# Four graph layers on one core: layer 2's clamp on POOL, and its next square between two exponentials

## The chip, the cores and the metric

The program runs on one core of a Trainium2 chip. The core has a matrix engine (TensorE, PE in the profile), a vector engine (VectorE, DVE), an engine for activation functions (ScalarE, ACT), a general engine (GpSimd, POOL) and an engine whose queue issues most transfers here (SyncE, SP). Each has its own instruction stream, works in order, and waits on semaphores for the others. [...] the large tiles of this kernel lie in SBUF.

The metric is the device time of one launch in microseconds (us), lower is better.

## The reference

Four layers are applied to x (4096 rows of 64) with one adjacency matrix adj (4096 by 4096). Each layer normalises the rows, cuts them at zero, calls a graph layer and adds its result to x. Layer 0 is a sum over neighbours with a linear map. Layer 1 is a Lorentz attention. Layer 3 weighs each neighbour by powers of one half according to its rank in the row. The change is in layer 2, where every pair of rows (i, j) needs the logarithmic map on the Poincare ball:

```python
sub = mobius_add(-x_i, x_j)
arg = clip(norm(sub), 0, 1 - 1e-5)
log_ij = 2 / lam_i * arctanh(arg) * sub / norm(sub)
agg = einsum('ij,ijc->ic', adj / deg, log_ij)
out = expmap(0, agg @ weight + bias)
```

The kernel takes a weight per pair, arctanh(arg)/norm(sub), out of a quantity that one set of matrix products gives for all pairs. It writes the arctanh as a logarithm. In layer 2 each pair therefore needs a square, a clamp from below, a square root, a logarithm, an inverse square root and a product with adj.

## The kernel before

The columns of adj are cut into 8 blocks of 512 (ib), and the 4096 rows into 16 groups of 256 (g, or J and half). A group is one tile of 128 partitions by 1024 elements: two chunks of 128 rows, each by 512 columns. The distance in layer 2 is symmetric, so only the groups on and above the diagonal are worked through: the list `work` has 72 groups. Row 0 has 16 of them, row 1 has 14, and so on down to 2 in row 7. Of these, 56 are used twice (`d["two"]`): once as they are, and once transposed by TensorE for the mirrored block, whose part is collected in the tile `others`. At each diagonal block the first group is whole and the second (`d["cut"]`) is half a tile.

One group k of layer 2 goes through these steps (the name of the generator, its engine, and the tiles by which the profile shows it):

- `l2_dists`, TensorE: matrix products into a PSUM pair tile (mm<-RT,LT and mm<-RB,LB). There are two such pair tiles.
- `l2_squares`, ScalarE: the square, from PSUM into a buffer v (v<-mm).
- `l2_clamps` (line 1032), VectorE: v = max(v - half, V_MIN), in place (v<-v, TENSOR_SCALAR).
- `l2_signs`, TensorE: two small products into the same PSUM tile, once the square has been read.
- `l2_roots` (line 1050), ScalarE: Ln of v in place (v<-v), Exp with factor 0.5 into a buffer t (t<-v), which is the root, and Exp with factor -0.5 in place (v<-v), which is the inverse root.
- `l2_coshs`, VectorE: t = max(PSUM, ...) + t (t<-mm,t). With this the PSUM pair tile is free.
- `l2_logs`, ScalarE: Ln of t in place (t<-t).
- `l2_pairs`, VectorE: t = min(t, top) * v (t<-t,v).
- `l2_weights`, VectorE: w = t * adj (w<-t,adj). `l2_turns`, TensorE: eight transposes (tr<-ident,t). `l2_weights2`, VectorE: two products (w<-tr,adj) of 512 elements each.
- `l2_sums` and `l2_sums2`, TensorE: the sums over neighbours (acc<-w,HA; 128x512 and 128x256 forms). `l2_gathers` adds the mirrored part to `others` after every second group: on VectorE in rows 1 to 7 (others<-acc,others), on ScalarE in row 0.

The buffers v and t come out of six buffers in turn, so three groups can be under way. All of these are recorded at one line (129) of the profile, by a helper, so the steps are told apart by their tiles.

At the end of each row, `after2` (line 613) turns the sums into the row's output, with small steps on all engines: a power on POOL (r_nn), a tanh on ScalarE between two loads of its table, and then the layer norm of layer 3 (`before3`, line 532) with another power (ln_r) and an addition (x<-x,b) on POOL. In row 0 layer 2's own preparations for later rows (`before2`) run beside the groups. Layer 3 begins while the last rows of layer 2 run: `l3_masks` makes its masks on VectorE.

The order of instructions on each engine is not written by hand. `in_turn` (line 709) holds a list of generators. Each yields the engine of its next step and a function that says when its inputs are ready. A class `Pace` (line 59) keeps an estimate of each engine's time; the generator that could start first goes next. `in_steps` binds several generators into one fixed order: in each step it takes them in the order given, each with its own shift in the number of the group. What the planner emits is kept in that order on each engine, and then runs whenever the semaphores allow. So a step put in another place moves others as well.

In the kernel before, ScalarE's order for group k is: Ln, Exp(0.5), Exp(-0.5), the square of group k+1, and the last Ln of k. VectorE's is: the clamp of k+1, the pair of k, the weight of k, the root's cosh step of k+1 and the two transposed weights of k, with `others` among them.

Of the kernel before, what the change touches and what calls it, by code (L numbers as in the profile page):

```python
# [14 lines left out]
ALU = mybir.AluOpType  # L15
# [35 lines left out]
V_MIN = 2.0**-64  # L51
# [85 lines left out]
def kernel(ctx: ExitStack, tc: tile.TileContext, a: dict, out: bass.AP):  # L137
# [5 lines left out]
    PE, DVE, ACT, POOL = (  # L143
        InOrder(tc, e, pace, name)
        for e, name in (
            (nc.tensor, "PE"), (nc.vector, "DVE"), (nc.scalar, "ACT"), (nc.gpsimd, "POOL"),
        )
    )
# [557 lines left out]
    def latest(*times):  # L706
        return None if None in times else max(times)
# [93 lines left out]
    def pair_buffer(name):  # L801
        return pairp.tile([P, G, W], F32, tag="pair", name=name)
# [148 lines left out]
    half = 0.25 * SC * SC  # L951
# [16 lines left out]
    def part(d, t):  # L968
        return t[:, :, OWN:] if d["cut"] else t
# [1 line left out]
    def targets(d):  # L971
        return slice(d["ib"] * W + (OWN if d["cut"] else 0), (d["ib"] + 1) * W)


    def ago(items, k, n, what):

        return items[k - n].get(what) if k >= n else 0.0
# [44 lines left out]
    def l2_squares():  # L1022
        for k, d in enumerate(work):
            yield "ACT", lambda: latest(
                d.get("dist"), l1[2 * k - SIG].get("summed") if 2 * k < SIG else 0.0,
                ago(work, k, SIG // 2, "paired"),
            )
            d["v"] = pair_buffer("v")
            ACT.activation(part(d, d["v"]), part(d, d["ps"]), AF.Square)
            d["square"] = pace.latest  # L1030

    def l2_clamps():
        for d in work:
            yield "DVE", lambda: d.get("square")
            v = part(d, d["v"])
            DVE.tensor_scalar(v, v, -half, V_MIN, ALU.add, ALU.max)
            d["clamped"] = pace.latest

    def l2_signs():
# [10 lines left out]
    def l2_roots():  # L1050
        for k, d in enumerate(work):
            yield "ACT", lambda: latest(
                d.get("clamped"), opened.get("tables"),
                l1[2 * k + 1 - SIG].get("summed") if 2 * k < SIG else 0.0,
                ago(work, k, SIG // 2, "weighed"), ago(work, k, SIG // 2, "turned"),
            )
            d["t"] = pair_buffer("t")
            v = part(d, d["v"])
            ACT.activation(v, v, AF.Ln)
            ACT.activation(part(d, d["t"]), v, AF.Exp, scale=0.5)  # L1060
            d["root"] = pace.latest
            ACT.activation(v, v, AF.Exp, scale=-0.5)
            d["inverse"] = pace.latest

# [7 lines left out]
    def l2_logs():  # L1072
        for d in work:
            yield "ACT", lambda: d.get("read")
            ACT.activation(part(d, d["t"]), part(d, d["t"]), AF.Ln, scale=2.0 / SC)
            d["log"] = pace.latest

    def l2_pairs():
        for d in work:
            yield "DVE", lambda: latest(d.get("log"), d.get("inverse"))  # L1080
            t = part(d, d["t"])
            DVE.scalar_tensor_tensor(t, t, top, part(d, d["v"]), ALU.min, ALU.mult)
            d["paired"] = pace.latest

    def l2_weights():
        for k, d in enumerate(work):
            yield "DVE", lambda: latest(
                opened.get("second"), d.get("paired"), arrival(d), ago(work, k, 2, "summed")
            )
            if not d["cut"]:  # L1090
                d["w"] = w2["pool"].tile([P, G, W], F32, tag="w", name="w")
            DVE.tensor_mul(part(d, d["w"]), part(d, d["t"]), part(d, d["adj"]))
            d["weighed"] = pace.latest
            used(d)
# [104 lines left out]
    def l2_gathers():  # L1199
        for d in twos:  # L1200
            if d["half"] == 0:
                continue
            yield "DVE" if d["ib"] else "ACT", lambda: d.get("summed2")
            o, acc = w2["others"][:, ws(d["J"])], accs["turned"][0 : D + 1, :]
            if d["ib"] == 0:
                ACT.copy(o, acc)
            else:
                DVE.tensor_add(o, acc, o)
            st["acc_free"][1] = pace.latest
            d["gathered"] = pace.latest  # L1210

    def in_steps(*stages):


        parts = [next(stage[0], None) for stage in stages]
        for step in range(-1, len(work) + 3):
            for n, (gen, behind, many) in enumerate(stages):
                k = step - behind
                for _ in range(many(work[k]) if 0 <= k < len(work) else 0):
                    yield parts[n]  # L1220
                    parts[n] = next(gen, None)
# [55 lines left out]
    def l3_masks():  # L1277
        for k, d in enumerate(l3):
            place, reader = mask_at[k % len(mask_at)]
            yield "DVE", lambda: latest(  # L1280
                arrival(d), reader.get("signed"), ago(l3, k, len(mask_at), "ranked")
            )
            d["m"] = place
            DVE.tensor_scalar(place, d["adj"], 0.0, None, ALU.not_equal)
            d["masked"] = pace.latest
            used(d)
# [7 lines left out]
    def l3_counts():  # L1294


        totals = []
        for h in range(2 * NB):
            half = l3[h * HG : (h + 1) * HG]
            yield "PE", lambda: latest(*(d.get("masked") for d in half)) if spare else None  # L1300
            ps = bank()
            for k in range(KH):
                for r in range(4):
                    c = 4 * k + r
                    PE.matmul(
                        ps[r * Q : (r + 1) * Q, :], pick[:, k, :],
                        half[::-1][c // G]["m"][:, c % G, :],
                        start=(k == 0), stop=(k == KH - 1), skip_group_check=True,
                    )
            yield "DVE", lambda: ready(ps)  # L1310
            totals = (totals if h % 2 else []) + [(1 - h % 2, l3_copy(f"total{h % 2}", ps))]
            yield "PE", lambda: ready(totals[-1][1]) if spare else None
            ps = bank()
            for n, (i, t) in enumerate(totals):
                PE.matmul(
                    ps, spread[:, i, :, :].rearrange("p q c -> p (q c)"), t,
                    start=(n == 0), stop=(n == len(totals) - 1),
                )
            yield "DVE", lambda: latest(ready(ps), ago(l3, h * HG, HG + 1, "ranked"))
            chunks = l3_copy("chunks", ps)  # L1320
            for d in half:
                d["chunks"] = chunks
# [31 lines left out]
    def l3_pass():  # L1354

        for n, pair in enumerate(pairs3):
            while rank_need(pair) is None:
                yield "PE", lambda: first_of(rank_need(pair), sum_need() if sums3 else None)
                if rank_need(pair) is None:
                    l3_sum()  # L1360
            yield "PE", lambda: rank_need(pair)
            l3_rank(pair)
            for _ in range(1 + n % 2):
                if sums3 and sum_need() is not None:
                    yield "PE", sum_need
                    l3_sum()
        while sums3:
            yield "PE", sum_need
            l3_sum()

    def l3_weights():
        n = 0
        for d in l3:
            if d["late"]:
                place, reader = late_at[d["k"]]
                yield "ACT", lambda: latest(d.get("ranked"), reader.get("signed"))
                d["w"] = place
            else:
                yield "ACT", lambda: latest(
                    d.get("ranked"), opened.get("third"),  # L1380
                    ago([e for e in l3 if not e["late"]], n, WT, "summed"),
                )
                d["w"] = now["w3"].tile([P, G, W], BF16, tag="wt", name="wt")
                n += 1
            ACT.activation(d["w"].bitcast(U16), d["ps"], AF.Relu)
            d["read"] = pace.latest
# [8 lines left out]
    def l3_sum():  # L1395
# [22 lines left out]
        if d["last"]:  # L1418
# [8 lines left out]
            (l2_dists(), -1, once), (l2_signs(), 0, once), (l2_sums2(), 2, if_two(1)),  # L1427
            (l2_turns(), 1, lambda d: 2 if d["two"] else 1), (l2_sums(), 1, once),
        ),
        in_steps((l2_logs(), 1, once), (l2_roots(), 0, once), (l2_squares(), -1, once)),  # L1430
        in_steps(
            (l2_clamps(), 0, once), (l2_pairs(), 1, once), (l2_weights(), 1, once),
            (l2_coshs(), 0, once), (l2_weights2(), 1, lambda d: 2 if d["two"] else 1 if d["first"] else 0),
        ),
        l2_gathers(), l3_weights(), l3_pass(), l3_counts(), l3_masks(),
        degree_sums(0, l0), degree_sums(1, l1), constants(),
    ])

# [44 lines left out]
```

## Time and profile before

| what | value |
|---|---|
| time, median of 3 runs | 1198.92 us (1196.69 to 1200.99) |
| the profiled execution's own time | 1196.08 us |
| span of its trace (first to last instruction) | 1194.4 us |
| mean granted TensorE clock | 0.978 of full speed |
| busy: PE / DVE / ACT / POOL | 1077.9 / 950.6 / 800.7 / 118.2 us |
| 487 to 592 us (row 0 of layer 2): PE / DVE / ACT busy of 105 | 95.8 / 94.2 / 92.1 us |
| 592 to 957 us (rows 1 to 7): PE / DVE / ACT busy of 365 | 318.9 / 333.6 / 291.3 us |
| 957 to 1194 us (mostly layer 3): PE / DVE / ACT busy of 237 | 213.9 / 117.6 / 132.7 us |

Layers 0 and 1 fill the first 485 us. The powers r_nn at the row ends of layer 2 start at 604.3, 692.0, 767.9, 832.2, 886.3, 930.3 and 960.3 us on POOL, which makes the rows visible.

In a timeline, a line begins with start and duration in us, then the engine, the line of the kernel, the operation, output<-input, the shapes and the number of instructions merged. In brackets stand the idle time before it and the instruction that ended it. Durations overlap a little: a VectorE instruction of 1.22 us is followed by the next one after 1.13 to 1.15 us, since the end of one runs beside the start of the next.

### The profile page before, as it was taken

What the parts mean: (1) busy time and instruction counts of PE and PEld (TensorE: products, weight loads), DVE (VectorE), ACT (ScalarE), POOL (GpSimd) and SP (SyncE); (2) the same over time, 40 slices, a digit from 0 to 9 for tenths busy, and PEclk for the clock granted to TensorE, in tenths of its full rate; (3) what the DMA queues carried; (4) which work ended last, traced back from release to release, by engine and by line L of the source; (5) the groups of instructions that cost most, each with busy time, mean ns of one, the idle gap of its engine ahead of it and who ended that gap; (6) DMA issues with size and microseconds to landing.
All of it is one profiled execution on the core that took longest, in us unless ns stands there. A gap on an engine that the chain in (4) does not pass through costs nothing.

```text
span 1194.4 us, 15545 instructions
## 1 busy us (share of the span) xinstructions
PE 1077.9 (90%) x5367; PEld 445.8 (37%) x5392; DVE 950.6 (80%) x1571; ACT 800.7 (67%) x1266; POOL 118.2 (10%) x99
## 2 busy tenths in 40 slices
PE   4799999999999999899979979899878779999997
PEld 1234443333333333244434434344433333333332
DVE  7889888869988887698989989898989884555550
ACT  1055456677776766879888798788876675555554
POOL 3123222002000010000010010100010120000000
PEclk9899999999999999899999999999999899999999
DMA  8899999775767764544535535344444398888830
GB/s 307 300 409 388 405 386 329 265 244 184 249 225 244 253 241 157 193 141 159 194 106 177 176 109 198 117 159 159 159 143 141 138 357 319 314 315 310 309 112 9
DMA packets 77190, 271.75 MB, mean 228 GB/s; under 512 B 10040, under 2 KB 11064, under 8 KB 77112
## 3 DMA queue, kind: packets, MB, share of 16 engines
q1 hardware_dynamic: 75456, 270.57, 63.7%
q8 instruction: 42, 0.69, 0.2%
q10 hardware_dynamic: 1656, 0.20, 0.1%
q14 instruction: 36, 0.29, 0.1%
HBM read 269.68 MB, written 1.05 MB: 227 GB/s over the span
## 4 chain that ended last, share of the span: by engine, by line
PE 47%; DVE 25%; ACT 13%; issue 7%; DMA 5%; POOL 2%; SPq 0%; ACTq 0%; DVEq 0%; POOLq 0%
PE acc L129 23%; PE mm L129 16%; PE tr L129 8%; DVE t L129 6%; DVE w L129 6%; DVE dg L129 4%; DMA adj<-in_adjT_dram 4%; ACT wt L129 3%; ACT v L129 3%; ACT t L129 2%; DVE v L129 1%; DVE sig L129 1%; POOL lo_s L129 1%; ACT sig L129 1%; ACT lo_sq L129 1%
## 5 line engine op out<-in xcount | busy, mean ns | idle before, releaser
L129 PE MATMUL acc<-w,HA 128*65 128x256 f32 (+1 forms) x736 | 252.6, 479 | 22.2 <-DVE w L129 13.8
L129 ACT ACTIVATE wt<-mm 128x1024 uint16<-128x1024 f32 x124 | 120.4, 1020 | 93.0 <-PE mm L129 93.0
L129 ACT ACTIVATE v<-v 128x1024 f32<-128x1024 f32 (+1 forms) x144 | 145.3, 1009 | 54.5 <-DVE v L129 52.2
L129 ACT ACTIVATE sig<-mm,att_b,att_a 128x1024 f32<-128x1024 f32 x128 | 148.5, 1202 | 44.2 <-PE mm L129 43.2
L129 DVE TENSOR_TENSOR sig<-sig,adj 128x1024 f32<-128x1024 f32 x128 | 152.5, 1220 | 28.3 <-ACT sig L129 28.1
L129 PE MATMUL acc<-adj,HA 128*64 128x512 f32 x512 | 128.0, 631 | 22.9 <-DVE HA L129 19.4
L129 DVE TENSOR_TENSOR dg<-dg,adj 128x1024 f32<-128x1024 f32 x114 | 139.1, 1220 | 2.0 <-DMA adj<-in_adjT_dram 0.6
L129 PEld LDWEIGHTS acc<-w,HA 128*65 128x65 f32 x736 | 95.8, 140 | 110.5 <-issue 59.5
L129 PE MATMUL mm<-qT,kT 64*128 64x512 f32 x512 | 132.6, 632 | 3.3 <-ACT sig L129 3.3
L129 PE MATMUL acc<-sig,HL 128*64 128x512 f32 x512 | 123.5, 605 | 1.6 <-DVE sig L129 1.5
L129 PE MATMUL acc<-wt,S 128*128 128x512 bf16 (+1 forms) x480 | 98.7, 391 | 2.7 <-issue 2.4
L129 DVE SCALAR_TENSOR_TENSOR t<-t,v 128x1024 f32<-128x1024 f32 x72 | 85.4, 1186 | 5.2 <-ACT t L129 5.2
L129 DVE SCALAR_TENSOR_TENSOR t<-mm,t 128x1024 f32<-128x1024 f32 x72 | 83.3, 1157 | 4.1 <-ACT t L129 2.1
L129 DVE TENSOR_TENSOR w<-tr,adj 128x512 f32<-128x512 f32 x120 | 78.5, 683 | 10.1 <-PE tr L129 10.1
L129 DVE TENSOR_TENSOR w<-t,adj 128x1024 f32<-128x1024 f32 x72 | 83.5, 1160 | 1.2
L129 PE MATMUL tr<-ident,t 128*128 128x128 f32 x480 | 67.7, 283 | 16.7 <-DVE w L129 6.9
L129 PE MATMUL mm<-RT,LT 64*128 64x512 f32 (+1 forms) x288 | 78.9, 625 | 3.6 <-DVE t L129 3.6
L129 ACT ACTIVATE t<-t 128x1024 f32<-128x1024 f32 x72 | 72.1, 1002 | 13.3 <-DVE t L129 13.2
L129 DVE TENSOR_SCALAR RT<-adj 128x1024 bf16<-128x1024 f32 x74 | 50.4, 696 | 33.5 <-PE mm L129 31.6
L129 ACT ACTIVATE t<-v 128x1024 f32<-128x1024 f32 x72 | 72.7, 1010 | 2.3
L129 PEld LDWEIGHTS mm<-qT,kT 64*128 64x128 f32 x512 | 43.9, 189 | 75.1 <-ACT sig L129 35.2
L129 ACT ACTIVATE v<-mm 128x1024 f32<-128x1024 f32 x72 | 69.2, 961 | 0.8 <-PE mm L129 0.8
(204 smaller groups left out, 1298.4 us busy)
## 6 DMA issues: line engine op xcount, KB each, us to landing
adj<-in_adjT_dram SPq DMA_DIRECT2D x512, 512.0 KB, 4.9
x<-in_x_dram SPq DMA_DIRECT2D x4, 256.0 KB, 3.8
out_dram<-h SPq DMA_DIRECT2D x8, 128.0 KB, 2.8
b<-in_b_dram ACTq DMA_DIRECT2D x2, 32.0 KB, 5.3
W<-in_W_dram ACTq DMA_DIRECT2D x3, 16.0 KB, 4.2
W0T<-in_W0T_dram ACTq DMA_DIRECT2D x2, 16.0 KB, 5.5
W1T<-in_W1T_dram ACTq DMA_DIRECT2D x1, 16.0 KB, 4.9
W1T<-in_b_dram ACTq DMA_DIRECT2D x1, 0.2 KB
```

The lines of the kernel that those rows point to most:

```text
L129: done = self.tc.keep_in_program_order(getattr(self.engine, op)(*args, **kw))
```

## The change

The clamp goes from VectorE to POOL, and its generator out of the fixed order that it shared with the pair, the weight and the cosh step; it runs as a generator of its own. The second exponential (the inverse root) gets a generator of its own, `l2_inverses`, which stands after the square in ScalarE's fixed order. No arithmetic changes.

```diff
     def l2_clamps():
         for d in work:
-            yield "DVE", lambda: d.get("square")
+            yield "POOL", lambda: d.get("square")
             v = part(d, d["v"])
-            DVE.tensor_scalar(v, v, -half, V_MIN, ALU.add, ALU.max)
+            POOL.tensor_scalar(v, v, -half, V_MIN, ALU.add, ALU.max)
             d["clamped"] = pace.latest
...
             ACT.activation(part(d, d["t"]), v, AF.Exp, scale=0.5)
             d["root"] = pace.latest
+
+    def l2_inverses():
+        for d in work:
+            yield "ACT", lambda: d.get("root")
+            v = part(d, d["v"])
             ACT.activation(v, v, AF.Exp, scale=-0.5)
             d["inverse"] = pace.latest
...
-        in_steps((l2_logs(), 1, once), (l2_roots(), 0, once), (l2_squares(), -1, once)),
         in_steps(
-            (l2_clamps(), 0, once), (l2_pairs(), 1, once), (l2_weights(), 1, once),
+            (l2_logs(), 1, once), (l2_roots(), 0, once), (l2_squares(), -1, once),
+            (l2_inverses(), 0, once),
+        ),
+        in_steps(
+            (l2_pairs(), 1, once), (l2_weights(), 1, once),
             (l2_coshs(), 0, once), (l2_weights2(), 1, lambda d: 2 if d["two"] else 1 if d["first"] else 0),
         ),
-        l2_gathers(), l3_weights(), l3_pass(), l3_counts(), l3_masks(),
+        l2_clamps(), l2_gathers(), l3_weights(), l3_pass(), l3_counts(), l3_masks(),
```

In the program that results, ScalarE's order for a group in the middle of a row is: Ln of k (which now waits for POOL), Exp(0.5) of k, the square of k+1, Exp(-0.5) of k, the last Ln of k. VectorE's is: pair of k, weight of k, cosh step of k+1, `others` (after every second group), two transposed weights of k. TensorE's order within such a group, and the order of transfers on SP, are as before. At a row end POOL has one clamp, r_nn, one clamp, ln_r, x<-x,b and then the next clamps.

## The prediction

> **What bounds the kernel now.** I read the busy table by stage first. Only 487 to 957 us (layer 2) is touched. There TensorE works 95.8 of 105 us in row 0 and 318.9 of 365 us in rows 1 to 7, so it is idle for 9 + 46 = 55 us: no gain inside layer 2 can pass that. VectorE is as full (94.2 and 333.6).
>
> Then the timeline of TensorE alone, in row 0:
>
> ```profile
> 550.95 1.94 PE L129 MATMUL acc<-w,HA 128*65 128x256 f32 x8
> 552.73 1.04 PE L129 MATMUL tr<-ident,t 128*128 128x128 f32 x8
> 553.60 1.88 PE L129 MATMUL acc<-w,HA 128*65 128x512 f32 x4
> 555.41 1.13 PE L129 MATMUL mm<-RT,LT 64*128 64x512 f32 x4
> 556.47 0.39 PE L129 MATMUL mm<-RB,LB 32*128 32x512 bf16 x4
> ```
>
> No idle time is shown, and the next group's acc<-w,HA starts at 556.80: a group costs TensorE 5.85 us, back to back. I take that as its floor. In row 1 every second group has a wait:
>
> ```profile
> 638.40 1.91 PE L129 MATMUL acc<-w,HA 128*65 128x256 f32 x8 [0.27 <-DVE others L129]
> 640.15 1.04 PE L129 MATMUL tr<-ident,t 128*128 128x128 f32 x8
> 641.02 1.88 PE L129 MATMUL acc<-w,HA 128*65 128x512 f32 x4
> ```
>
> The period there alternates between 6.15 (717.62 - 711.47, two clamps) and 5.85 (723.47 - 717.62).
>
> Third, one such period on VectorE and the ScalarE step that waits for it:
>
> ```profile
> 717.62 0.68 DVE L129 TENSOR_SCALAR v<-v 128x1024 f32<-128x1024 f32 x1
> 718.22 1.22 DVE L129 SCALAR_TENSOR_TENSOR t<-t,v 128x1024 f32<-128x1024 f32 x1
> 718.34 1.06 ACT L129 ACTIVATE v<-v 128x1024 f32<-128x1024 f32 x1 [1.06 <-DVE v L129]
> 719.48 1.22 DVE L129 TENSOR_TENSOR w<-t,adj 128x1024 f32<-128x1024 f32 x1
> 720.62 1.22 DVE L129 SCALAR_TENSOR_TENSOR t<-mm,t 128x1024 f32<-128x1024 f32 x1
> 722.26 1.29 DVE L129 TENSOR_TENSOR w<-tr,adj 128x512 f32<-128x512 f32 x2 [0.43 <-PE tr L129]
> ```
>
> By start-to-start times VectorE spends 0.60 (clamp) + 1.14 + 1.14 + 1.13 + 1.21 = 5.22 us, and 5.82 with `others` (0.60). Mid-row, TensorE and VectorE bind together.
>
> Last, the chain of waits through the row end at 768 us. It runs almost wholly over VectorE and ScalarE, and the clamp is on it:
>
> ```profile
> 759.58 0.62 DVE v L129
> 760.19 0.02 issue
> 760.22 1.07 ACT v L129
> ...
> 768.94 3.25 DMA adj<-in_adjT_dram
> ...
> 782.09 0.67 DVE v L129
> ```
>
> **What the Trainium skill says.** "SBUF — State Buffer", section "SBUF: two separate sides": GpSimd and VectorE share one pair of ports as an exclusive lock, which a VectorE operation with two SBUF inputs, or in a two-port mode, takes against a GpSimd operation. The trace agrees:
>
> ```profile
> 699.95 0.73 POOL L129 TENSOR_TENSOR x<-x,b 128x256 f32<-128x256 f32 x1
> 700.04 1.72 DVE L129 SCALAR_TENSOR_TENSOR t<-t,v 128x1024 f32<-128x1024 f32 x1 [0.25 <-ACT t L129]
> ```
>
> The same t<-t,v takes 1.22 us alone: it lost 0.50. At 938.78 us the POOL addition took 1.26 instead of 0.73, beside a VectorE TENSOR_SCALAR. "GPSIMD Engine Reference", "Engine selection", calls a one-input elementwise operation there roughly line-rate. No POOL row of the trace is such an operation at this size.
>
> **The change, part by part.**
>
> *Removed from VectorE:* 72 clamps, 64 of 684 ns and 8 of 415 ns, 47.1 us busy, about 0.60 us of stream each.
>
> *Added to POOL:* the same 72. Bounds for one of 1024 elements: POOL's memsets take 0.206, 0.313 and 0.524 us for 128, 256 and 512, thus 0.10 + 0.83 ns per element: 0.95 us, the lower end. Two inputs of 256 take 0.73 us; with 0.22 of it fixed (0.73 less the 0.50 that VectorE lost), 1024 elements would take 0.22 + 4 x 0.50 = 2.2 us: the upper end, since this has one input. The affine select (128 elements in 0.30) gives 0.10 + 1024 x 1.6 ns = 1.7. I take 1.3, near line-rate, and keep 0.95 to 2.2.
>
> *What hides it:* the square of k+1 now ends before Exp(-0.5) of k and the last Ln of k, which is 2 x 1.05 = 2.1 us before ScalarE wants the clamped v. ScalarE has five steps of about 1.05 us, 5.25, in a period of 5.85, so another 0.6. Up to 2.1 us the clamp costs nothing, up to about 2.7 us it only uses slack, and beyond that every group pays the excess. Queued behind this Ln are the root, the next square and, through them, the cosh step and TensorE's PSUM tile.
>
> *The lock:* mid-row, the clamp falls beside the cosh step and the transposed weights, which have one input in PSUM and one in SBUF, so it meets no second SBUF input. The pair follows about 2 us after the square. No cost there; at a row end, where the order shifts, one collision of 0.5 us each: 7 x 0.5 = 3.5 us. If the mid-row cover fails, it is up to 0.5 to 1 us a group.
>
> *Mid-row, rows 1 to 7:* 42 groups are used twice, so 21 have `others`. VectorE needs 4.62 or 5.22 us without the clamp, and `others` no longer stands behind clamp and pair, so the wait goes and TensorE's 5.85 is what remains: 21 x 0.30 = 6.3 us. Row 0 copies `others` on ScalarE and is on TensorE's floor already: nothing.
>
> *Row ends:* between 755 and 790 us five clamps leave VectorE, 5 x 0.6 = 3.0 us, while its idle time there is about 4 us. Ln at 760.22 waited 2.29 us for a clamp that stood behind after2's steps. Following the new order by hand with these durations, the cosh step of 762.39 comes 1.0 us earlier (its clamp gone and its root no longer late). The weight that ends at 768.92, and lets go the buffer that the 3.25 us transfer waits for, comes 1.7 us earlier, and the cosh step at 785.08 about 2.5 us. Moving Exp(-0.5) behind the two table loads gives back some of it, included. I take 2.5 a row end, between 0 (if the transfer or ScalarE sets it) and 4.4 (TensorE's idle time in the 12 us from 692, 12 - 7.6): 7 x 2.5 = 17.5 us.
>
> *Start of row 0:* the chain has clamps at 494.16, 506.04, 512.36 and 527.71 us: 4 x 0.6 = 2.4 us. After 528 it goes over ScalarE, which gains nothing.
>
> *POOL's queue:* r_nn (2.49 us) and ln_r (1.01) now stand between clamps. Before r_nn the clamp's square lies ahead of the table loads, so it is done; the clamp behind r_nn belongs to a square behind the tanh that waits for r_nn itself. I count nothing; without that cover it is 2.5 us a row end. SP's order is unchanged: its transfers move with the buffers. Layer 3 (957 us on) only starts earlier.
>
> Sum: 6.3 + 17.5 + 2.4 - 3.5 = 22.7 us. The profiled execution took 1196.08 us (span 1194.4), so 1173; it lies 2.8 under the median, against which I forecast 1198.9 - 22.7 = 1176.
>
> **Rivals.**
>
> *Row ends do not move.* For: the transfer (3.25 us) and the two table loads (2 x 1.28) remain on the chain. Against: the buffer's release depends on VectorE steps that come earlier. The mid-row part and the start remain: 6.3 + 2.4 = 8.7 us, 1190.
>
> *More at the row ends.* The hand-followed order reaches over 4 us at `others` (789.22), where the clamp of 787.49 also goes. With 4.4 each and no collisions, 30.8 + 8.7: 1160.
>
> *Slower: POOL becomes the wait.* If a clamp takes over 2.7 us from square to Ln, the excess is paid 72 times. It decides at 2.7 + 22.7/72 = 3.0 us; at 3.3 us, 72 x 0.6 - 22.7 makes it 1219. For: the powers show POOL software far from line-rate (2.45 us for 8 elements), and a clamp that first waits for a pair's lock loses 1.2 us. Against: memset, select and addition all stay below 2.2.
>
> *No change.* TensorE's floor or a lower granted clock (0.978 now) takes what VectorE frees. For: row 0 is at the floor. Against: 46 us of idle TensorE after it.
>
> **From cases to numbers.** Around 1176 (own range 1168 to 1185): 0.55. Row ends unmoved, 1185 to 1195: 0.17. More, below 1168: 0.15. No change, within 0.3% (3.6 us, about what a measurement can tell): 0.04. Slower: 0.09. Faster is 0.55 + 0.17 + 0.15 = 0.87. The range 1160 to 1194 leaves out the slower case, no change and the ends of two others.
>
> **What would show it.** Right: POOL's v<-v at 1.0 to 2.2 us; few ScalarE waits for it; TensorE's period at 5.85 in rows 1 to 7 with no wait for `others`; the r_nn powers around row 1 some 83 us apart (87.7 - 6 x 0.3 - 2.5), not 87.7; t<-t,v still near 1.22 us. Wrong: t<-t,v or w<-t,adj at 1.7 or more on average (lock), ScalarE's Ln waiting for POOL in most groups, or row ends as long as before though the clamp left them.

## The result, and the profile after

| | before | changed |
|---|---|---|
| time, median (range) | 1197.81 us (1196.58 to 1200.99), 4 runs | 1239.78 us (1237.33 to 1244.2), 4 runs |
| ratio, 95% interval | | 1.0345 [1.0313, 1.0377] |
| profiled execution, span | 1196.08, 1194.4 us | 1244.2, 1242.5 us |
| mean granted TensorE clock | 0.978 | 0.95 |

The changed kernel is 3.5% slower. The forecast was 1176. The outcome is the rival "POOL becomes the wait".

The first line of the page after, busy time by engine:

```profile
PE 1107.6 (89%) x5367; PEld 460.8 (37%) x5392; DVE 924.8 (74%) x1499; ACT 797.2 (64%) x1266; POOL 371.3 (30%) x171
```

VectorE lost 25.8 us and POOL gained 253.1. POOL's share is still the smallest of the four, so this line alone would not name it. The instructions of the tile v (shortest / median / longest in ns) give the price of one clamp, and the page's costliest groups give who waits:

```profile
L129 POOL TENSOR_SCALAR v<-v x72: 1919/3627/5452, 484.7 to 989.4; 128x1024 f32<-128x1024 f32 x64, 128x512 f32<-128x512 f32 x8
```

```profile
L129 POOL TENSOR_SCALAR v<-v 128x1024 f32<-128x1024 f32 x72 | 252.3, 3504 | 244.1 <-ACT v L129 237.4
L129 ACT ACTIVATE v<-v 128x1024 f32<-128x1024 f32 (+1 forms) x144 | 144.7, 1005 | 93.1 <-POOL v L129 92.0
```

A clamp of 1024 elements mostly takes 3.63 us and one of 512 takes 1.92. The last column is idle time: POOL waits for ScalarE (237.4 us), and ScalarE waits for POOL (92.0 us). Two engines that each wait for the other form a closed loop, and the timeline of the changed kernel in the middle of row 2 shows it:

```profile
738.93 3.63 POOL L129 TENSOR_SCALAR v<-v 128x1024 f32<-128x1024 f32 x1 [3.17 <-ACT v L129]
740.91 1.21 DVE L129 SCALAR_TENSOR_TENSOR t<-t,v 128x1024 f32<-128x1024 f32 x1
...
742.60 1.06 ACT L129 ACTIVATE v<-v 128x1024 f32<-128x1024 f32 x1 [1.85 <-POOL v L129]
743.69 1.06 ACT L129 ACTIVATE t<-v 128x1024 f32<-128x1024 f32 x1
744.65 1.01 ACT L129 ACTIVATE v<-mm 128x1024 f32<-128x1024 f32 x1
...
745.74 3.63 POOL L129 TENSOR_SCALAR v<-v 128x1024 f32<-128x1024 f32 x1 [3.17 <-ACT v L129]
```

The clamp of k+1 lets Ln of k+1 start. Behind it ScalarE does Exp(0.5) and then the square of k+2, and only this square lets the next clamp start. One turn is 3.63 us on POOL and 3.17 on ScalarE, 6.80 us (745.74 - 738.93). TensorE needs 5.85. The chain of work that ended last, between 738 and 753 us, is this loop and nothing else. The 3.13 us of "issue" are the three ScalarE steps, which this view does not name:

```profile
738.93 3.63 POOL v L129
742.56 3.13 issue
...
745.74 3.63 POOL v L129
```

Where the 48.1 us of span came from can be read at the powers r_nn, which mark the row ends. There are eight; the first seven start at 621.75, 719.07, 804.26, 875.89, 934.21, 983.72 and 1007.30 us, the eighth at 1021.73 (before: 974.87). Against the kernel before, row 0 ends 17.5 us later, 1.0 of which it has from a later start of layer 2; the five intervals behind it grew by 9.6, 9.3, 7.4, 4.2 and 5.5 us, the sixth shrank by 6.4, and the part behind the seventh power grew by 1.1. In row 1 the loop explains most of the 9.6 us: ten clamps in a row stand 61.3 us apart from the first to the last (634.71 to 696.03), nine turns of 6.8, where the same ten stood 52.9 us apart before (618.52 to 671.40), so 8.4 us. TensorE's clock is not the cause: from 735 to 785 us it was granted at 1.00, and the period there is 6.80 all the same.

### The profile page after: what moved, and what is told of

Same layout as the page of the kernel before. It is cut to its first block, busy times and chain, and to the rows that moved or that the text cites. A ratio compares the mean times of both kernels' runs of the same rounds, so it can differ in the third digit from the quotient of the medians.

```text
span 1242.5 us, 15622 instructions
## 1 busy us (share of the span) xinstructions
PE 1107.6 (89%) x5367; PEld 460.8 (37%) x5392; DVE 924.8 (74%) x1499; ACT 797.2 (64%) x1266; POOL 371.3 (30%) x171
## 4 chain that ended last, share of the span: by engine, by line
PE 38%; POOL 19%; issue 16%; DVE 13%; ACT 11%; DMA 3%; ACTq 0%; SPq 0%; POOLq 0%; DVEq 0%
PE acc L129 17%; POOL v L129 16%; PE mm L129 14%; PE tr L129 7%; DVE dg L129 3%; ACT wt L129 3%; ACT v L129 2%; DMA adj<-in_adjT_dram 2%; DVE w L129 2%; ACT t L129 1%; DVE t L129 1%; DVE sig L129 1%; POOL lo_s L129 1%; ACT sig L129 1%; ACT lo_sq L129 1%
## 5 line engine op out<-in xcount | busy, mean ns | idle before, releaser
L129 POOL TENSOR_SCALAR v<-v 128x1024 f32<-128x1024 f32 x72 | 252.3, 3504 | 244.1 <-ACT v L129 237.4
L129 PE MATMUL acc<-w,HA 128*65 128x256 f32 (+1 forms) x736 | 274.9, 514 | 24.5 <-DVE w L129 17.6
L129 PEld LDWEIGHTS acc<-w,HA 128*65 128x65 f32 x736 | 103.2, 151 | 124.9 <-issue 67.5
L129 PE MATMUL mm<-RT,LT 64*128 64x512 f32 (+1 forms) x288 | 82.9, 654 | 32.6 <-DVE t L129 32.3
L129 POOL TENSOR_TENSOR ln_r<-ln_v,minus_half 128x4 f32<-128x4 f32 x32 | 49.9, 1559 | 129.9 <-DVE ln_v L129 129.9
```

The lines of the kernel that those rows point to most:

```text
L129: done = self.tc.keep_in_program_order(getattr(self.engine, op)(*args, **kw))
```

## The experiments

Theory A: the closed loop through POOL costs the time, because a clamp takes 3.63 us. Theory B: ScalarE's new order costs it, with the inverse root a step later for the pair and the square a step earlier. Theory C: the lock between POOL and VectorE, of which the prediction speaks, costs it, whatever the order. The diffs are against the changed kernel.

### The new order on ScalarE alone

The clamp is back on VectorE in its old place; the square stays between the exponentials.

```diff
-            yield "POOL", lambda: d.get("square")
+            yield "DVE", lambda: d.get("square")
...
-            POOL.tensor_scalar(v, v, -half, V_MIN, ALU.add, ALU.max)
+            DVE.tensor_scalar(v, v, -half, V_MIN, ALU.add, ALU.max)
...
-            (l2_pairs(), 1, once), (l2_weights(), 1, once),
+            (l2_clamps(), 0, once), (l2_pairs(), 1, once), (l2_weights(), 1, once),
...
-        l2_clamps(), l2_gathers(), l3_weights(), l3_pass(), l3_counts(), l3_masks(),
+        l2_gathers(), l3_weights(), l3_pass(), l3_counts(), l3_masks(),
```

> Only the new place of the second exponential (after the next square); the clamp stays on VectorE in its old place. Theory A (a closed loop: POOL's clamp of 3.63 us, then Ln, Exp and the next square, 3.17 us, then the next clamp, sets 6.80 us a group): without POOL in the loop the loss is gone, and the earlier square may even help a little: 1185 to 1202 us. Theory B (the new order on ScalarE costs by itself, at the row ends above all, where the exponential now stands behind two table loads): most of the loss stays, 1225 us or more.

Measured: 1196.94 us (1192.73 to 1200.01), before on the same chip 1197.39, ratio 0.9991 [0.9974, 1.0007]. The order costs nothing and brings nothing by itself. Theory B falls.

### The clamp on POOL, in the old order on ScalarE

```diff
-        in_steps(
-            (l2_logs(), 1, once), (l2_roots(), 0, once), (l2_squares(), -1, once),
-            (l2_inverses(), 0, once),
-        ),
+        in_steps((l2_logs(), 1, once), (l2_roots(), 0, once), (l2_inverses(), 0, once), (l2_squares(), -1, once)),
```

> Only the clamp on POOL; ScalarE does Ln, both exponentials and then the square, as before. Theory A: the second exponential enters the loop, 3.63 + 4.26 = 7.89 us a group, 1.09 us more than in the changed kernel, some 60 groups mid-row: about 1305 us. Theory B: the loss goes with the order, 1200 us or less. Theory C (POOL's port lock against VectorE, whatever the order): about 1240, as in the changed kernel.

Measured: 1309.06 us (1304.52 to 1313.03), ratio 1.0913 [1.0873, 1.0952]. The timeline of this kernel in row 1:

```profile
699.81 3.63 POOL L129 TENSOR_SCALAR v<-v 128x1024 f32<-128x1024 f32 x1 [4.26 <-ACT v L129]
703.47 1.06 ACT L129 ACTIVATE v<-v 128x1024 f32<-128x1024 f32 x1 [2.80 <-POOL v L129]
...
706.61 1.01 ACT L129 ACTIVATE v<-mm 128x1024 f32<-128x1024 f32 x1
707.69 3.63 POOL L129 TENSOR_SCALAR v<-v 128x1024 f32<-128x1024 f32 x1 [4.26 <-ACT v L129]
```

With a fourth ScalarE step in the loop (the inverse root, ahead of the square) a turn takes 7.88 us, 1.08 more than in the changed kernel. Over 72 groups that is 78 us as an estimate; the medians differ by 69. The new order on ScalarE is thus worth 69 us once the clamp is on POOL, and nothing without it. That is near theory A's 1305; B expected 1200 or less, and C about 1240.

### The clamp's arithmetic left out

The clamp is computed on no engine: neither the subtraction of half nor the bound is done, so the logarithm sees the bare square. The order on ScalarE is the changed kernel's.

```diff
-            yield "POOL", lambda: d.get("square")
-            v = part(d, d["v"])
-            POOL.tensor_scalar(v, v, -half, V_MIN, ALU.add, ALU.max)
-            d["clamped"] = pace.latest
+            yield "ANY", lambda: d.get("square")
+            pace.latest = d["square"]
+            d["clamped"] = pace.latest
```

> As the changed kernel, with the clamp left out on every engine (the subtraction of half and the lower bound are not computed, so the square goes straight to Ln). It shows what the change could bring at most if POOL's clamp cost nothing. Theory A1 (the sum of the prediction without its lock term is right, only POOL's price was mis-sized): 26 us less than before, about 1171 us, with the row ends some 2.5 us shorter each. Theory A2 (the row ends do not follow VectorE's relief, since ScalarE's two table loads, the power, and the transfer set them): only mid-row and start, 8.7 us, about 1189, and a row end as long as before.

Measured: 1177.67 us (1173.78 to 1178.98), before on the same chip 1197.55, ratio 0.9819 [0.979, 0.9849]. That is 19.9 us below before, nearer to the 26 of theory A1 than to the 8.7 of A2. It is the worth of a clamp that costs nothing anywhere. The chain of work that ended last, 638 to 645 us of this kernel:

```profile
638.12 1.39 PE mm L129 x8
639.51 1.87 PE acc L129 x8
641.38 0.87 PE tr L129 x8
...
643.97 1.39 PE mm L129 x8
```

It lies on TensorE alone, with a period of 5.85 us (643.97 - 638.12), in groups with `others` and without.

### One operation in place of two

The subtraction is moved into ScalarE's logarithm, as its bias, and POOL only takes a maximum.

```diff
+    minus_h = const.tile([P, 1], F32, name="minus_h")
+    POOL.memset(minus_h, -0.25 * SC * SC)
...
-            POOL.tensor_scalar(v, v, -half, V_MIN, ALU.add, ALU.max)
+            POOL.tensor_scalar(v, v, half * (1 + 2.0**-23), None, ALU.max)
...
-            ACT.activation(v, v, AF.Ln)
+            ACT.activation(v, v, AF.Ln, bias=minus_h)
```

> As the changed kernel, but POOL's clamp has one operation instead of two: it takes the maximum with the next number above half, and ScalarE's Ln takes half off as its bias. If POOL's price goes by the operations on an element, the clamp takes about 2 us instead of 3.63, the loop 5.2 us, below TensorE's 5.85: theory A then expects 1176 to 1190 us, the gain that was forecast. If the price is that of the instruction (3.6 us whatever its operations), theory A expects no change, about 1240. Theory B and C: 1225 or more at either price.

Measured: 1193.57 us (1190.07 to 1196.74), ratio 0.9962 [0.9946, 0.9978]. The timeline of this kernel in row 1:

```profile
639.51 2.77 POOL L129 TENSOR_SCALAR v<-v 128x1024 f32<-128x1024 f32 x1 [3.26 <-ACT v L129]
642.31 1.15 ACT L129 ACTIVATE v<-v,minus_h 128x1024 f32<-128x1024 f32 x1 [0.99 <-POOL v L129]
643.49 1.06 ACT L129 ACTIVATE t<-v 128x1024 f32<-128x1024 f32 x1
644.45 1.01 ACT L129 ACTIVATE v<-mm 128x1024 f32<-128x1024 f32 x1
645.54 2.77 POOL L129 TENSOR_SCALAR v<-v 128x1024 f32<-128x1024 f32 x1 [3.27 <-ACT v L129]
```

This is 0.4% under the kernel before and misses theory A's 1176 to 1190. A is right in kind and wrong in size: the number expected took some 2 us for the clamp, and it takes 2.77. The turn is 6.03 us, 0.18 over TensorE's 5.85. The logarithm's bias is paid in the same loop: 1.15 us for 1.06. That agrees with the Trainium skill, "ScalarE: Activation LUTs", "What ACT_TABLE_LOAD costs", by which a per-partition pointer operand adds about 93 ns. Taking 0.86 us out of the clamp (3.63 - 2.77) gave back 46 of the 1239.8 us: the POOL clamp's duration sets the time.

### The square still earlier on ScalarE

The square of k+1 goes ahead of Ln of k, so the loop is opened: the clamp of k+1 now runs beside Ln and both exponentials of k.

```diff
-            (l2_logs(), 1, once), (l2_roots(), 0, once), (l2_squares(), -1, once),
-            (l2_inverses(), 0, once),
+            (l2_logs(), 1, once), (l2_squares(), -1, once), (l2_roots(), 0, once),
+            (l2_inverses(), 0, once),
```

> As the changed kernel, but ScalarE squares group k+1 ahead of Ln of group k, so a clamp has some five ScalarE steps (about 5 us) before its Ln, and the loop spans two groups. POOL's 3.63 us stays as it is. Theory A: it is hidden, the period goes back to TensorE's 5.85, 1176 to 1195 us (a square that waits for its PSUM tile may take some of it). Theory C (lock): no better than the changed kernel, 1235 or more, as POOL does as much. Theory B: no better either, since the second exponential is still late.

Measured: 1205.23 us (1202.7 to 1207.33), ratio 1.0064 [1.0046, 1.0082]. The timeline of this kernel in row 1:

```profile
642.91 1.03 ACT L129 ACTIVATE v<-mm 128x1024 f32<-128x1024 f32 x1 [0.55 <-PE mm L129]
643.65 1.23 DVE L129 TENSOR_TENSOR w<-t,adj 128x1024 f32<-128x1024 f32 x1
...
644.02 4.34 POOL L129 TENSOR_SCALAR v<-v 128x1024 f32<-128x1024 f32 x1 [1.52 <-ACT v L129]
...
648.77 1.03 ACT L129 ACTIVATE v<-mm 128x1024 f32<-128x1024 f32 x1 [0.46 <-PE mm L129]
```

Theories B and C expected no better than the changed kernel (C 1235 or more), and both fall again; A's 1176 to 1195 is missed too. ScalarE no longer waits for POOL here, though the clamp grew to 4.34 us: mid-row, opening the loop takes the slow clamp off the path. But the square now waits about half a microsecond in every group for its PSUM tile. The period shown is 5.86 us and alternates with 5.96, 5.91 in the mean, and row 1 takes 89.1 us against 87.7 before. With both edits together, this order and the single operation:

> The wider window (square of k+1 ahead of Ln of k) together with POOL's single operation (2.77 us alone, half taken off by Ln's bias). With the wider window the two-operation clamp took 4.35 to 4.44 us, since it met VectorE's two-input steps, and the period was 5.95. With one operation the clamp should take 2.8 to 3.6 us and have over 1 us to spare. If POOL still set anything in the wider order, this is faster than it by up to 8 us (1197); if the wider order itself is what costs (the square waits 0.5 us a group for its PSUM tile, the row ends are longer), it stays at 1202 to 1207.

Measured: 1207.93 us (1206.91 to 1212.45), ratio 1.0074 [1.0049, 1.0098]. A cheaper clamp brings nothing in this order, so the clamp's duration is not what costs the 8 and 10 us over before. In row 1 the mean period grew from 5.91 to 6.00 us, by as much as the bias adds to Ln, which speaks for a path over ScalarE. Row 0 ended 3.5 and 4.6 us later than before. The clamp still lengthens VectorE's w<-t,adj in this order (1.34 us in the mean for 1.22), and no run has this order with the clamp on VectorE, so the order's share and POOL's were not taken apart.

### Half a clamp on POOL

POOL clamps the first 512 elements, VectorE the other 512.

```diff
-            POOL.tensor_scalar(v, v, -half, V_MIN, ALU.add, ALU.max)
-            d["clamped"] = pace.latest
+            POOL.tensor_scalar(v[:, 0], v[:, 0], -half, V_MIN, ALU.add, ALU.max)
+            d["clamped0"] = pace.latest
+
+    def l2_clamps2():
+        for d in work:
+            yield "DVE", lambda: latest(d.get("square"), d.get("clamped0"))
+            v = part(d, d["v"])
+            DVE.tensor_scalar(v[:, 1], v[:, 1], -half, V_MIN, ALU.add, ALU.max)
+            d["clamped"] = pace.latest
...
-            (l2_pairs(), 1, once), (l2_weights(), 1, once),
+            (l2_clamps2(), 0, once), (l2_pairs(), 1, once), (l2_weights(), 1, once),
```

> The clamp is cut in two: POOL clamps the first 512 elements of each partition, VectorE the second 512 in the clamp's old place. POOL's part takes 1.92 us (as measured for the half tiles), so the loop is 1.92 + 3.17 = 5.1 us, below TensorE's 5.85, and VectorE gives up 0.27 of 0.60 us a group. Theory A: no loss, mid-row at 5.85 to 5.95, 1185 to 1197 us. Theory C (POOL's work on the shared ports hurts by itself): above 1200.

Measured: 1200.58 us (1192.93 to 1204.42), ratio 1.0011 [0.9994, 1.0028]. Theory A's 1185 to 1197 is missed. The sum hides two parts. From the first r_nn to the seventh it is 347.3 us (964.19 - 616.93) against 356.0 before (960.31 - 604.29): rows 1 to 6 gained 8.8 us. But row 0 ended 12.6 us later, at 616.93. Most of that can be read at TensorE, which waited twice there, 4.61 and 3.68 us, for ScalarE's copy of `others`:

```profile
555.77 0.57 ACT L129 COPY others<-acc 65x512 f32<-65x512 f32 x1
556.39 3.68 PE L129 MATMUL acc<-w,HA 128*65 128x256 f32 x8 [4.61 <-ACT others L129]
```

In the kernel before TensorE has no such wait. Here the planner put the copy behind five ScalarE steps of the next group (550.93 to 554.83). The changed kernel has 5.3 us of these waits in row 0, and the kernel without the clamp one of 5.13, so it takes no clamp on POOL to make them.

### POOL helps only from row 1 on

In row 0 VectorE clamps the whole tile, as before; in rows 1 to 7 the clamp is shared as above, or is POOL's single operation (there, VectorE's clamp in row 0 is the single maximum too, with the bias in Ln). The ScalarE order is the changed kernel's in all rows. The edit of the first:

```diff
+    def l2_clamps0():
+        for d in work:
+            if d["ib"]:
+                continue
+            yield "DVE", lambda: d.get("square")
+            v = part(d, d["v"])
+            DVE.tensor_scalar(v, v, -half, V_MIN, ALU.add, ALU.max)
+            d["clamped"] = pace.latest
...
     def l2_clamps():
         for d in work:
+            if d["ib"] == 0:
+                continue
...
-            (l2_pairs(), 1, once), (l2_weights(), 1, once),
+            (l2_clamps2(), 0, lambda d: d["ib"] > 0), (l2_clamps0(), 0, lambda d: d["ib"] == 0), (l2_pairs(), 1, once), (l2_weights(), 1, once),
```

> As the split clamp (512 elements on POOL, 512 on VectorE), but only in rows 1 to 7; in row 0 VectorE clamps the whole tile as in the kernel before. In the split kernel the end of row 0 came 12.6 us later than before (616.9 against 604.3), while the seven intervals after it were 8.3 us shorter in sum. If both hold by themselves, this is some 8 us faster than before, about 1189 us; if the later rows were short only because row 0 had been late (transfers further ahead, say), no gain.

Measured: 1187.92 us (1183.87 to 1195.36), before on the same chip 1198.76, ratio 0.9913 [0.9885, 0.994]. Row 0 ends at 603.18, and the seventh r_nn starts 348.2 us behind it: the gain in rows 1 to 6 does not need the loss in row 0.

> As the single operation on POOL (2.77 us, half in Ln's bias), but only in rows 1 to 7; row 0 is clamped by VectorE. The end of row 0 came 4.3 us later than before with POOL there (608.6 against 604.3). If that is POOL's loop in row 0, this gains up to 4 us on it, about 1190 us.

Measured: 1188.66 us (1187.14 to 1190.68), ratio 0.9913 [0.9882, 0.9943]. Both are 0.9% faster than the kernel before. In neither does TensorE wait for the copy of `others` in row 0. Why the planner puts that copy later when row 0's clamp is not VectorE's alone was not tested, nor were the other 4 us that row 0 lost in the shared form.

## Why the prediction was wrong

**The step that failed is POOL's price**, in "Added to POOL": "I take 1.3, near line-rate, and keep 0.95 to 2.2", with the upper end from a two-input addition, "since this has one input". Measured: 3.63 us for 1024 elements and 1.92 for 512, thus 3.34 ns per element and 0.21 us fixed. The fixed part was right (0.22). What was wrong is that the number of inputs bounds the price per element. The single maximum takes 2.77 and 1.49 us, 2.50 ns per element, so the second arithmetic operation costs another 0.83 ns: the operations count too. Even one operation on one input is dearer than the 1.95 ns (0.50 us for 256) that the prediction read for an addition of two. The Trainium skill's "roughly line-rate" for one input ("GPSIMD Engine Reference", "Engine selection") isn't seen here, neither with one operation nor with two; VectorE did both on this tile in 0.68 us. The rows of the trace below 2.2 us that spoke "against" the slower rival were no such operations: a memset reads nothing, the addition does one operation, and the select is another instruction, measured at 128 elements only.

**The slack was right.** The prediction had the clamp free up to 2.1 us and paid in full beyond "about 2.7". The loop gives 5.85 - 3.17 = 2.68 us. With the measured 3.63 the rival's own sum is 72 x (3.63 - 2.7) - 22.7 = +44, thus 1243; the median is 1239.8. That the sum comes so near has some luck in it, for it counts eight half tiles as whole. A better check is the kernel without a clamp: the changed one is 62.1 us slower (1239.78 - 1177.67), and 64 whole clamps at 3.63 - 2.68 make 61. Mechanism, place and threshold of the slower rival hold, and its chance was set at 0.09 because of the price. The sign it named, Ln waiting for POOL in most groups, came: 57 waits in 72 groups.

**The gain that was hoped for exists, if the clamp is free.** The kernel without a clamp lies 19.9 us under before, where 22.7 were forecast. By its parts, profiled run against profiled run: from the first r_nn to the seventh, 330.0 us for 356.0, so 26.0, where mid-row (6.3) and six row ends (15.0) were to give 21.3. In row 1 it is 3.8 us (83.9 for 87.7, "some 83" was forecast), but not where it was forecast. "In row 1 every second group has a wait" was misread: in the kernel before only two groups of row 1 have it, this one and the 0.27 that the prediction shows.

```profile
626.40 1.91 PE L129 MATMUL acc<-w,HA 128*65 128x256 f32 x8 [1.15 <-DVE others L129]
```

The 6.15 and 5.85 were read between clamps near the start of row 2; TensorE's own period in row 1 is 5.85 from 644.22 on. In rows 1 to 7 these waits are 8.1 us, in nine places. They are gone without the clamp, but from the third to the twelfth of these products row 1 takes 52.8 us in both kernels. The stretch ahead of that, with the 1.15, became 0.7 us shorter, and the row's end, from the twelfth to the next r_nn, 3.1 us (9.6 for 12.8). So row 1 had 0.7 for the 1.8 mid-row and 3.1 for the 2.5 at its end; that the sum came near is luck in part. The rival "row ends do not move" falls with that.

The term "start of row 0", 2.4 us, did not show: row 0 ended 2.0 us later without the clamps, at 606.28, though layer 2 began 2.9 us earlier. The 5.13 us wait for the copy of `others` stands in between, so the term itself was not tested. Another 1.8 us were lost behind the seventh r_nn (235.9 us for 234.1). That run has no lock on POOL and no clamp in POOL's queue, so it does not test those two terms.

**The lock mid-row costs nothing, but not for the reason given.** The clamp was to meet no second SBUF input. In the timeline of row 2 the pair t<-t,v, which has two, runs inside the clamp, and it stayed at 1.22 us all the same (the last section has more). At the row ends the term was too small: at five of the eight, ln_xc lost 0.7 us and ln_v 0.6, against one collision of 0.5. Whether these set the time was not isolated.

**POOL's queue was not free.** "Before r_nn the clamp's square lies ahead of the table loads, so it is done" fails with the long clamp. The timeline of the changed kernel at the end of row 1:

```profile
715.48 3.63 POOL L129 TENSOR_SCALAR v<-v 128x1024 f32<-128x1024 f32 x1 [4.78 <-ACT v L129]
...
717.74 0.17 DVE L129 COPY r_nn<-r_nn 128x4 f32<-128x4 f32 x1
...
719.07 1.82 POOL L129 TENSOR_TENSOR r_nn<-r_nn,halves 128x8 f32<-128x8 f32 x1
```

The power's input was ready at 717.91, and it started 1.16 us later, when the clamp ended. It took 1.82 us for the 2.49 of before, so its result came 0.5 us later than it would have with no clamp ahead and before's duration. This is small beside the loop.

**"No change" fell.** TensorE's floor is real (5.85 in the run without a clamp), but rows 1 to 7 held time above it, around the row ends.

## What to carry to other kernels

Price an operation on another engine at its own form, number of operations and size; where the trace has no such row, put the upper end where the change would turn harmful, and ask whether anything measured excludes it. Count the closed loop (the moved step, and what must run before its next input exists) against the period, not only the slack to the next waiter. A slow helper can still pay where it gets a share that brings its loop near or under the bound: here half a tile, or one operation for two, and only in rows 1 to 7.

## What the runs showed of the hardware

- POOL's tensor_scalar in f32, in place, 128 partitions: with two operations 1.06 us for 256 elements, 1.92 for 512, 3.63 for 1024; with one, 1.49 and 2.77.
- The lock between POOL and VectorE depends on when they meet. In the timeline of the middle of row 2 above, the pair t<-t,v has two SBUF inputs and ran from 740.91 to 742.12, wholly inside the clamp of 738.93 to 742.56; neither took longer than elsewhere. The Trainium skill ("SBUF — State Buffer", "SBUF: two separate sides") has the lock held for a whole instruction; for this one-input POOL operation the records show otherwise. At the start of a clamp it is felt, and for one step at its end. The timeline of the changed kernel near a row end:

```profile
725.22 3.63 POOL L129 TENSOR_SCALAR v<-v 128x1024 f32<-128x1024 f32 x1 [4.33 <-ACT v L129]
725.41 1.13 DVE L129 SCALAR_TENSOR_TENSOR ln_xc<-ln_m,x 128x256 f32<-128x256 f32 x1
...
728.10 0.78 DVE L129 TENSOR_SCALAR ln_v<-ln_v 128x4 f32<-128x4 f32 x1
```

  The ln_xc step, issued 0.19 us into the clamp, took 1.13 us where it takes 0.42 alone. The four-element ln_v step took 0.78 where it takes 0.17, and ended within 0.03 us of the clamp. The other way round, a clamp that starts behind the start of w<-t,adj is longer the sooner it comes: 4.05 us at 0.66 us behind it (706.65, changed kernel), 4.34 at 0.37 (644.02, the kernel with the earlier square, shown above) and 4.44 at 0.27 (649.88 there). Starts and ends on POOL are rough in these records, and when exactly the lock is held was not tested.
